# Light attention by whole token tiles, and a clock rule with fitted weights in the planner

## The chip, the core and the metric

The kernel runs on one core of a Trainium2 chip. A core has TensorE (PE; its weight loads are shown as PEld), VectorE (DVE), ScalarE (ACT), GpSimd (POOL) and SyncE (SP, which issues most DMAs). TensorE writes into PSUM, eight banks of 128 partitions by 512 float32 columns; VectorE or ScalarE copy the results out ("evict" them) into SBUF before TensorE can use them as operands or a bank can take the next tile. The metric is the device time of one execution in microseconds; the time of a kernel is the median of several executions.

## The reference

A macaron block on `x` of 8 sequences, 1024 tokens, 256 features, all float32: half a mixture of experts, attention, half a mixture of experts again.

```python
x = x + 0.5 * ffn(layernorm(x))
x = x + attn(layernorm(x))
x = x + 0.5 * ffn(layernorm(x))

def ffn(x):                      # 8 experts, hidden 128, the best two of each token
    logits = x @ router_w + router_b
    w = top-2 of softmax(logits), normalised
    return sum over experts of w * (gelu(x @ W1 + b1) @ W2 + b2)

def attn(x):                     # 8 heads of 64
    # light: windows of 64 tokens, each looks at itself and its two neighbours
    q, k, v = split(layernorm(x) * ln_g + ln_b) @ wqkv_l
    light = softmax(q k^T / 8 over 192 keys) v @ wo_l
    # heavy: the 256 best tokens by x.rt_q look at the 256 best by x.rt_kv
    heavy = softmax(hq hk^T / 8) (hv) @ wo_h, put back at the queries' places
    return light + heavy
```

## The kernel before

All eight sequences go through three stages: the first experts, attention, the last experts. Sequence 0 (first experts) and sequence 7 (last experts) compute all eight experts for every token (`dense`); the others sort their tokens by expert in DRAM, gather them in slots of 128 (`xp`, an indirect DMA from GpSimd), fetch the slot's expert weights (`wt`, 256 KB from SyncE) and compute one expert for a slot: transposes into `pt`, eviction to `xTe`, first layer into `ph`, GELU into `act`, second layer into `po`, eviction to `yp`. Different sequences' stages run at once: while one is in attention, others are in their experts.

Light attention (`light`, L1895) goes over 8 tiles of 128 tokens (two windows) of a sequence and, for each, over two groups `g` of four heads. `scores_light` (L1486) multiplies queries and keys of a group into `sim` (a tile of two PSUM banks, two such tiles take turns) with matmuls on 64 by 64 parts of the array, and `soften` (L1408) makes the softmax: negative maximum on VectorE (`nmax`), four exponentials on ScalarE (`a`, with sums `asum`), a reciprocal, and the scaling of `a` on VectorE or GpSimd. `values_light` (L1523) then works on one group: four transposes of the window's own keys into `pa`, evicted to `at` (512 columns); two transposes of the other keys into half of a bank `pb`, evicted to `bt` (256 columns); the products with the values into half of a bank `pav`, the own keys on 128 by 64 parts of the array and the neighbours' on 64 by 64 parts; and the eviction of that half (256 columns) to `loT`. After both groups `finish` multiplies `loT` by the output weights (`lo`), adds `ha` and stores to `h_b`. The calls stand one group behind the scores: scores of a group, then values of the group before. `prepare(t+1)` loads the next tile's `ha` and the neighbours' values `vside`.

SBUF tiles are taken in turn from rings: pool `two` has two buffers for each tag, `three` three, `one` one (`Plan.pool`, L301). Four of the eight PSUM banks hold the `sim` tiles, the other four are given to all other tiles (`bank`).

The order of the instructions is not the program's order. The program is run once with every call recorded; a planner (`Plan`, from L289) builds the dependences, orders the recorded calls by a list schedule with a cost for each (`Op.cost`, `Engine.work`), picks the engine for evictions and scalings (`copy`, `affine`, `scale`) and the PSUM bank for each tile, and repeats this for some rounds with ranks from the end. `schedule` (L517) has a small model of TensorE's clock in `run` (L538): in windows of `GATE` = 3413 ns the clock is full or half, by the busy share of the window before; before the change every busy nanosecond counts alike:

```python
busy = clock[2] / GATE
clock[0] = 1.0 if busy > (0.93 if clock[0] < 1 else 0.52) else 0.5
```

The program's order matters for the rings and for the first ranks. It is set by `PLACES` (L77): every stage has a start and an end on a scale where sequence `b`'s light attention takes `b` to `b + 1`, and `PLACES` adds an offset to each. Because almost every call goes through the recorder, most instructions carry the line of its issue, L269; evictions that choose their engine carry L352, L362 to L367, scalings L377. Instructions are told apart by the names of their tiles.

Of the kernel before, what the change touches and what calls it, by code (L numbers as in the profile page):

```python
# [44 lines left out]
F32 = mybir.dt.float32  # L45
# [12 lines left out]
P = 128  # L58
# [18 lines left out]
PLACES = {  # L77
    0: (-0.182, -0.019),
    1: (0.014, 0.072),
    2: (0.088, 0.002),  # L80
    3: (0.444, -0.124),
    4: (-0.157, -0.245),
    5: (-0.045, -0.526),
    6: (0.377, -0.016),
    8: (-0.109, 0.000),
    9: (0.160, -0.078),
    10: (0.002, -0.129),
    11: (0.070, 0.254),
    12: (0.003, 0.003),
    13: (0.434, 0.082),  # L90
    14: (0.122, -0.024),
    15: (0.274, 0.222),
    16: (0.214, 0.139),
    17: (0.169, 0.000),
    18: (0.273, -0.045),
    19: (0.099, 0.049),
    20: (0.074, -0.435),
    21: (0.000, 0.117),
    22: (0.205, -0.014),
    23: (-0.072, -0.036),  # L100
    24: (-0.039, -0.018),
    25: (-0.013, 0.000),
    26: (0.055, 0.481),
    27: (-0.013, 0.068),
    28: (-0.016, 0.000),
    30: (0.000, 0.002),
    31: (0.000, 0.484),
    32: (0.000, 0.090),
    34: (-0.002, 0.015),
    36: (0.063, 0.000),  # L110
    37: (0.034, -0.012),
    38: (0.032, 0.032),
    39: (0.000, -0.362),
    40: (0.029, 0.010),
    41: (0.499, 0.498),
    42: (0.099, 0.231),
    43: (0.000, 0.020),
    44: (0.050, -0.164),
    45: (0.007, -0.066),
    46: (0.311, 0.028),  # L120
    47: (0.196, 0.228),
    48: (0.076, -0.023),
    49: (0.030, -0.083),
    50: (0.000, 0.068),
    51: (-0.049, -0.114),
    52: (0.025, 0.137),
    53: (0.005, -0.060),
    54: (0.066, -0.609),
    55: (0.019, -0.108),
    56: (0.030, 0.183),  # L130
    57: (0.236, 0.070),
    58: (0.064, 0.043),
    59: (0.047, -0.286),
    60: (0.034, 0.000),
    61: (0.050, 0.000),
    62: (-0.041, -0.014),
    63: (0.123, -0.043),
    64: (-0.124, -0.048),
    65: (-0.290, -0.365),
    66: (-0.097, 0.030),  # L140
    67: (0.024, -0.106),
    68: (-0.011, 0.032),
    69: (0.132, 0.030),
    70: (0.439, 0.061),
}

# [18 lines left out]
RATE = 270.0  # L165
TURN = 185
QUARTER = 29
GATE = 3413.0


# [59 lines left out]
class Engine:  # L230
# [43 lines left out]
    @staticmethod  # L274
    def work(method, out, ins, kw):

        rows, cols, n = ins[0].shape[0], free(ins[0]), free(out)
        if method == "transpose":
            return {"work": 109.5, "array": (128, 128)}
        if ins[0].dtype in (BF16, F16):  # L280
            return {"work": max(25, n / 2.4 + 5), "array": (128, 128)}
        array = (64 if rows <= 64 else 128, 64 if cols <= 64 else 128)
        if array == (64, 64):
            return {"work": 58 * n / 64, "array": array}
        t = max(n * 2 / 2.4, cols / 1.2) + 4
        return {"work": t if array != (128, 128) else 2 * t, "array": array}


class Plan:  # L289
# [227 lines left out]
    def schedule(self, before, after, rank):  # L517
# [17 lines left out]
        last_use = [0.0] * len(left)  # L535
        free_at = dict.fromkeys(range(self.banks), 0.0)

        def run(t, work):  # L538
            while work > 1e-6:
                while clock[1] + GATE <= t:  # L540
                    busy = clock[2] / GATE
                    clock[0] = 1.0 if busy > (0.93 if clock[0] < 1 else 0.52) else 0.5
                    clock[1] += GATE
                    clock[2] = 0.0
                step = min(work / clock[0], clock[1] + GATE - t)
                clock[2] += step
                t += step
                work -= step * clock[0]
            return t
# [28 lines left out]
        while len(result) < len(ops):  # L578
# [11 lines left out]
            if e == PE:  # L590
                changed = o.how["array"] != array
                array = o.how["array"]
                now[e] = run(t, takes + (TURN if changed else 0))
                done = now[e] + (170 if clock[0] == 1 else 230) + LATE
            else:
                now[e], done = t + takes, t + seen_after + LATE
# [125 lines left out]
def program(  # L722
# [200 lines left out]
    def bank(name):  # L923
        return pmm.tile([P, HALF], F32, name=name)
# [595 lines left out]
                score(*one_of)  # L1520
        return soften(sim, 3 * W, f"{n}_{g}")

    def values_light(a, vside, t, g, loT, n):  # L1523


        at = keys_first(a, OWN, f"{n}_{g}_0")

        pb = bank(f"pb_{n}_{g}")
        for c in range(2):
            pair = a[:, 2 * c : 2 * c + 2, :].rearrange("p j k -> p (j k)")  # L1530
            nc.tensor.transpose(pb[:, ts(c, P)], pair[:, P : 2 * P], ident)
        bt = two.tile([P, 2, P], F32, tag="bt", name=f"bt_{n}_{g}")
        evict(bt.rearrange("p c q -> p (c q)"), pb[:, : 2 * P])
        pav = bank(f"pav_{n}_{g}")
        beside = windows_beside(t)


        for c in range(2):
            for j in range(2):
                hh = (4 * g + 2 * c + j) * DH  # L1540
                nc.tensor.matmul(
                    pav[j * DH : (j + 1) * DH, ts(c, P)],
                    v[:, t, hh : hh + DH],
                    at[:, 2 * c + j, :],
                    start=(c == 0),
                    stop=False,
                )
# [17 lines left out]
        evict(loT[:, ts(g, 2), :].rearrange("p c q -> p (c q)"), pav[:, : 2 * P])  # L1565


    def pc_of(pr, i):
# [326 lines left out]
    def light(b):  # L1895
# [240 lines left out]
```

## Time and profile before

| | us |
|---|---|
| median of 6 runs | 1830.6 (1826.22 to 1843.93) |
| the profiled execution | 1832.0 |
| its span, first to last instruction | 1830.3 |
| TensorE, matmuls busy | 1676.4 |
| TensorE, weight loads busy (beside matmuls) | 1248.6 |
| VectorE busy | 1233.9 |
| ScalarE busy | 918.4 |
| GpSimd busy | 846.5 |

The mean clock granted to TensorE was 0.965 of full speed. Busy times are sums over one execution; engines work beside each other. In a group's line stand source line, engine, operation, output and inputs by the program's names, shapes, count, then busy time, mean nanoseconds of one, and idle time of the engine ahead of it with what ended it. In the tile names `atl` is light and `ath` heavy attention, `f` an expert stage, and the digit before it the sequence.

### The profile page before, as it was taken

To read this page: it belongs to the slowest core of one execution; us is meant where nothing else is said; L and a number is where in the kernel's file an instruction comes from. 1 tells how busy PE (TensorE), PEld (TensorE's weight loads), DVE (VectorE), ACT (ScalarE), POOL (GpSimd) and SP (SyncE) were. 2 spreads that over 40 slices of the span, in tenths; PEclk is the share of its full clock that TensorE was granted. 3 is DMA by queue.
4 is the path that set the end of the run, shared out by engine and by line. 5 is a ranking of instruction groups with operands and counts; after the bars stand their busy time and mean duration, and the time that the engine had idled before them with its cause. 6 is when DMAs were issued, how large, how long until landed. Compare 5 with 4: busy or idle time off the path is not lost.

```text
span 1830.3 us, 39317 instructions
## 1 busy us (share of the span) xinstructions
PE 1676.4 (92%) x13753; PEld 1248.6 (68%) x13753; DVE 1233.9 (67%) x3904; ACT 918.4 (50%) x2554; POOL 846.5 (46%) x733
## 2 busy tenths in 40 slices
PE   7899899999999998899999889889989998999897
PEld 5676567666767766667767566658767666677786
DVE  5778559873865486677556698648647695558746
ACT  1134456545755543555646345538636454455532
POOL 1054562464642235553565644546454635454433
PEclk8899899999999999999999999999989999999999
DMA  9467765244851234564775432537565425744264
GB/s 163 167 217 212 216 200 158 71 126 128 268 166 53 53 102 148 179 213 122 226 241 171 119 107 91 179 110 227 186 203 151 134 86 155 226 124 135 73 190 125
DMA packets 220134, 284.66 MB, mean 156 GB/s; under 512 B 53496, under 2 KB 160960, under 8 KB 219680
## 3 DMA queue, kind: packets, MB, share of 16 engines
q1 hardware_dynamic: 190992, 208.82, 36.7%
q0 software_dynamic: 28368, 73.31, 14.7%
q8 instruction: 109, 1.79, 0.4%
q14 instruction: 89, 0.73, 0.1%
q10 hardware_dynamic: 576, 0.02, 0.0%
HBM read 196.20 MB, written 80.61 MB: 151 GB/s over the span
## 4 chain that ended last, share of the span: by engine, by line
PE 71%; DVE 16%; issue 5%; ACT 2%; DMA 2%; another core or an unknown queue 2%; POOL 1%; DVEq 0%; POOLq 0%; SPq 0%; ACTq 0%
PE po_0f L269 3%; PE ph_0f L269 3%; PE po_2f L269 2%; PE po_6f L269 2%; PE po_4f L269 2%; PE ph_2f L269 2%; PE po_7f L269 2%; PE ph_7f L269 1%; PE ph_4f L269 1%; PE ph_6f L269 1%; PE pt_2f L269 1%; PE pt_4f L269 1%; PE pt_6f L269 1%; PE lo_6at L269 1%
## 5 line engine op out<-in xcount | busy, mean ns | idle before, releaser
L269 ACT ACT_TABLE_LOAD x89 | 114.2, 1283 | 2.7 <-DVE nmax_5atl L269 1.2
L269 POOL DMA_INDIRECT xp_2f<-y_2f,token_2f x78 | 82.6, 1059 | 63.2 <-PE pt_2f L269 24.2
L269 POOL DMA_INDIRECT xp_6f<-y_6f,token_6f x62 | 64.4, 1039 | 68.7 <-PE pt_6f L269 43.2
L269 POOL DMA_INDIRECT xp_4f<-y_4f,token_4f x62 | 67.4, 1087 | 41.1 <-PE pt_4f L269 14.8
L269 POOL DMA_INDIRECT xp_0f<-y_0f,token_0f x39 | 41.5, 1064 | 41.7 <-PE pt_0f L269 20.9
L269 PE MATMUL po_2f<-wt_2f,act_2f 128*128 128x256 f32 x156 | 47.5, 395 | 7.0 <-issue 5.4
L269 PEld LDWEIGHTS ph_2f<-xTe_2f,wt_2f 128*128 128x128 f32 x312 | 42.2, 198 | 6.0 <-issue 4.1
L269 PE MATMUL ph_2f<-xTe_2f,wt_2f 128*128 128x128 f32 x312 | 46.0, 284 | 0.0
L269 POOL DMA_INDIRECT xp_1f<-y_1f,token_1f x23 | 24.7, 1076 | 42.6 <-PE pt_1f L269 14.8
L269 DVE SCALAR_TENSOR_TENSOR x_last<-po_7f,weight_7f,x_last 128x256 f32<-128x256 f32 x64 | 28.4, 478 | 21.2 <-PE po_7f L269 18.7
L269 PE MATMUL po_0f<-experts,act_0f 128*128 128x256 f32 x128 | 37.0, 430 | 5.4 <-DVE x_0at L269 5.4
L269 ACT ACTIVATE act_0f<-ph_0f,b_sb 128x512 f32<-128x512 f32 x16 | 11.0, 688 | 57.6 <-PE ph_0f L269 57.6
L377 POOL TENSOR_TENSOR a_7atl<-a_7atl,asum_7atl 128x768 f32<-128x768 f32 x14 | 21.0, 1503 | 38.4 <-DVE asum_7atl L269 20.0
L377 POOL TENSOR_TENSOR a_2atl<-a_2atl,asum_2atl 128x768 f32<-128x768 f32 x10 | 14.8, 1475 | 50.4 <-DVE asum_2atl L269 31.9
L269 PEld LDWEIGHTS ph_4f<-xTe_4f,wt_4f 128*128 128x128 f32 x248 | 33.7, 195 | 6.2 <-issue 4.6
L269 PE MATMUL ph_4f<-xTe_4f,wt_4f 128*128 128x128 f32 x248 | 36.5, 282 | 1.3 <-issue 1.1
L269 PEld LDWEIGHTS po_0f<-experts,act_0f 128*128 128x128 f32 x128 | 27.0, 219 | 15.4 <-DVE x_0at L269 6.2
L269 PEld LDWEIGHTS po_2f<-wt_2f,act_2f 128*128 128x128 f32 x156 | 24.6, 198 | 18.2 <-issue 12.2
L269 PE MATMUL po_6f<-wt_6f,act_6f 128*128 128x256 f32 x124 | 35.9, 383 | 1.2 <-issue 1.2
L269 PE MATMUL ph_6f<-xTe_6f,wt_6f 128*128 128x128 f32 x248 | 35.0, 278 | 2.1 <-issue 1.3
L269 PEld LDWEIGHTS ph_6f<-xTe_6f,wt_6f 128*128 128x128 f32 x248 | 32.5, 191 | 6.3 <-issue 3.5
L269 PE MATMUL po_4f<-wt_4f,act_4f 128*128 128x256 f32 x124 | 36.7, 387 | 0.0
(1547 smaller groups left out, 5889.8 us busy)
## 6 DMA issues: line engine op xcount, KB each, us to landing
wt_2f<-wpk SPq DMA_DIRECT2D x78, 256.5 KB
wt_4f<-wpk SPq DMA_DIRECT2D x62, 256.5 KB
wt_6f<-wpk SPq DMA_DIRECT2D x62, 256.5 KB
wt_0f<-wpk SPq DMA_DIRECT2D x39, 256.5 KB
ys_2f<-yp_2f SPq DMA_DIRECT2D x38, 256.0 KB
ys_4f<-yp_4f SPq DMA_DIRECT2D x30, 256.0 KB
ys_6f<-yp_6f SPq DMA_DIRECT2D x30, 256.0 KB
o<-h_b SPq DMA_DIRECT2D x56, 128.0 KB
```

The lines of the kernel that those rows point to most:

```text
L269: op = Op(self.plan, engines, lambda _: issue(*args, **kw), outs, ins, kind, **how)
L377: return getattr(nc, engine).tensor_tensor(dst, dst, by, op=ALU.mult)
```

## The change

`values_light` takes both groups of a token tile at once: `pb`, `bt` and `pav` hold all eight heads (512 columns), `loT` is evicted once; `at` stays one for each group. `bt` has one buffer in place of two. The planner's clock model gets a weight `live` for each kind of TensorE work (transposes 1.15, matmuls on parts of the array 1.0, small router matmuls 0.25, others by their columns), turns of the array count nothing, and the thresholds become 0.85 (to wake) and 0.5 (to keep). Most entries of `PLACES` have new values; the rings of SBUF buffers are as they were.

```diff
--- before.py
+++ after.py
@@ -77,70 +77,72 @@
...
-    2: (0.088, 0.002),
...
+    2: (0.093, 0.007),
...
-    12: (0.003, 0.003),
...
+    12: (-0.134, -0.134),
...
+    29: (0.005, 0.000),
...
-    39: (0.000, -0.362),
...
+    39: (0.158, -0.362),
...
-    65: (-0.290, -0.365),
...
+    65: (0.512, 0.433),
...
-    67: (0.024, -0.106),
-    68: (-0.011, 0.032),
...
+    67: (0.024, -0.354),
+    68: (0.069, -0.482),
...
@@ -165,6 +167,7 @@
 RATE = 270.0
 TURN = 185
 QUARTER = 29
+WAKES, KEEPS = 0.85, 0.5
 GATE = 3413.0
 
 
@@ -276,14 +279,18 @@
 
         rows, cols, n = ins[0].shape[0], free(ins[0]), free(out)
         if method == "transpose":
-            return {"work": 109.5, "array": (128, 128)}
+            return {"work": 109.5, "live": 1.15, "array": (128, 128)}
         if ins[0].dtype in (BF16, F16):
-            return {"work": max(25, n / 2.4 + 5), "array": (128, 128)}
+            work = max(25, n / 2.4 + 5)
+            return {"work": work, "live": n / 2.4 / work, "array": (128, 128)}
         array = (64 if rows <= 64 else 128, 64 if cols <= 64 else 128)
         if array == (64, 64):
-            return {"work": 58 * n / 64, "array": array}
+            return {"work": 58 * n / 64, "live": 1.0, "array": array}
         t = max(n * 2 / 2.4, cols / 1.2) + 4
-        return {"work": t if array != (128, 128) else 2 * t, "array": array}
+        if array != (128, 128):
+            return {"work": t, "live": 1.0, "array": array}
+        live = n * 4 / 2.4 / (2 * t) if n > 16 else 0.25
+        return {"work": 2 * t, "live": live, "array": array}
 
 
 class Plan:
@@ -535,15 +542,15 @@
         last_use = [0.0] * len(left)
         free_at = dict.fromkeys(range(self.banks), 0.0)
 
-        def run(t, work):
+        def run(t, work, live):
             while work > 1e-6:
                 while clock[1] + GATE <= t:
                     busy = clock[2] / GATE
-                    clock[0] = 1.0 if busy > (0.93 if clock[0] < 1 else 0.52) else 0.5
+                    clock[0] = 1.0 if busy > (WAKES if clock[0] < 1 else KEEPS) else 0.5
                     clock[1] += GATE
                     clock[2] = 0.0
                 step = min(work / clock[0], clock[1] + GATE - t)
-                clock[2] += step
+                clock[2] += step * live
                 t += step
                 work -= step * clock[0]
             return t
@@ -590,7 +597,7 @@
             if e == PE:
                 changed = o.how["array"] != array
                 array = o.how["array"]
-                now[e] = run(t, takes + (TURN if changed else 0))
+                now[e] = run(run(t, TURN if changed else 0, 0), takes, o.how["live"])
                 done = now[e] + (170 if clock[0] == 1 else 230) + LATE
             else:
                 now[e], done = t + takes, t + seen_after + LATE
@@ -1520,39 +1527,39 @@
                 score(*one_of)
         return soften(sim, 3 * W, f"{n}_{g}")
 
-    def values_light(a, vside, t, g, loT, n):
-
-
-        at = keys_first(a, OWN, f"{n}_{g}_0")
-
-        pb = bank(f"pb_{n}_{g}")
-        for c in range(2):
-            pair = a[:, 2 * c : 2 * c + 2, :].rearrange("p j k -> p (j k)")
-            nc.tensor.transpose(pb[:, ts(c, P)], pair[:, P : 2 * P], ident)
-        bt = two.tile([P, 2, P], F32, tag="bt", name=f"bt_{n}_{g}")
-        evict(bt.rearrange("p c q -> p (c q)"), pb[:, : 2 * P])
-        pav = bank(f"pav_{n}_{g}")
+    def values_light(both, vside, t, loT, n):
+
+        ats = [keys_first(a, OWN, f"{n}_{g}_0") for g, a in enumerate(both)]
+
+        pb = bank(f"pb_{n}")
+        for g, a in enumerate(both):
+            for c in range(2):
+                pair = a[:, 2 * c : 2 * c + 2, :].rearrange("p j k -> p (j k)")
+                nc.tensor.transpose(pb[:, ts(2 * g + c, P)], pair[:, P : 2 * P], ident)
+        bt = one.tile([P, KI, P], F32, tag="bt", name=f"bt_{n}")
+        evict(bt.rearrange("p c q -> p (c q)"), pb)
+        pav = bank(f"pav_{n}")
         beside = windows_beside(t)
 
 
-        for c in range(2):
+        for c in range(KI):
             for j in range(2):
-                hh = (4 * g + 2 * c + j) * DH
+                hh = (2 * c + j) * DH
                 nc.tensor.matmul(
                     pav[j * DH : (j + 1) * DH, ts(c, P)],
                     v[:, t, hh : hh + DH],
-                    at[:, 2 * c + j, :],
+                    ats[c // 2][:, 2 * (c % 2) + j, :],
                     start=(c == 0),
                     stop=False,
                 )
-        for c in range(2):
+        for c in range(KI):
             for w in beside:
                 for j in range(2):
                     r = slice(j * DH, (j + 1) * DH)
-                    hh = (4 * g + 2 * c + j) * DH
+                    hh = (2 * c + j) * DH
                     q = c * P + w * W
                     if w == j:
-                        vs = vside[r, 2 * g + c, :]
+                        vs = vside[r, c, :]
                     else:
                         vs = v[r, t + 2 * w - 1, hh : hh + DH]
                     nc.tensor.matmul(
@@ -1560,9 +1567,9 @@
                         vs,
                         bt[r, c, w * W : (w + 1) * W],
                         start=False,
-                        stop=(c == 1 and w == beside[-1]),
+                        stop=(c == KI - 1 and w == beside[-1]),
                     )
-        evict(loT[:, ts(g, 2), :].rearrange("p c q -> p (c q)"), pav[:, : 2 * P])
+        evict(loT.rearrange("p c q -> p (c q)"), pav)
 
 
     def pc_of(pr, i):
@@ -1942,22 +1949,21 @@
         prepare(0)
         waiting = None
         for t in range(NT):
+            assert written[0] == b and (t < 3 or written[1] == b)
+            if waiting is not None:
+                values_light(*waiting)
+                light_done[0] += 2
+                finish(t - 1, waiting[3])
+            both = [scores_light(t, g, f"{n}l{t}") for g in range(2)]
+            yield
+            if t + 1 < NT:
+                prepare(t + 1)
             loT = two.tile([P, KI, P], F32, tag="loT", name=f"loT_{n}_l{t}")
-            for g in range(2):
-                assert written[0] == b and (t < 3 or written[1] == b)
-                a = scores_light(t, g, f"{n}l{t}")
-                if waiting is not None:
-                    values_light(*waiting)
-                    light_done[0] += 1
-                    if g == 0:
-                        finish(t - 1, waiting[4])
-                if g == 0 and t + 1 < NT:
-                    prepare(t + 1)
-                waiting = (a, sides[t], t, g, loT, f"{n}l{t}")
-                yield
+            waiting = (both, sides[t], t, loT, f"{n}l{t}")
+            yield
         values_light(*waiting)
-        light_done[0] += 1
-        finish(NT - 1, waiting[4])
+        light_done[0] += 2
+        finish(NT - 1, waiting[3])
         if b not in EARLY:
             add_heavy(b, h_b[b])
         yield
```

More of the change, by code (lines that the diff above doesn't have):

```diff
@@ L79 @@
     1: (0.014, 0.072),
-    2: (0.088, 0.002),
-    3: (0.444, -0.124),
+    2: (0.093, 0.007),
+    3: (0.395, -0.124),
     4: (-0.157, -0.245),
     5: (-0.045, -0.526),
-    6: (0.377, -0.016),
+    6: (0.343, -0.122),
+    7: (0.000, -0.021),
     8: (-0.109, 0.000),
     9: (0.160, -0.078),
-    10: (0.002, -0.129),
-    11: (0.070, 0.254),
-    12: (0.003, 0.003),
[L90 to L97, printed above, removed]
+    10: (0.086, -0.129),
+    11: (0.079, 0.231),
+    12: (-0.134, -0.134),
+    13: (0.242, 0.043),
+    14: (0.266, 0.347),
+    15: (0.325, 0.193),
+    16: (0.293, 0.060),
+    17: (0.076, -0.108),
+    18: (0.203, -0.068),
+    19: (0.232, 0.090),
+    20: (0.152, -0.384),
     21: (0.000, 0.117),
-    22: (0.205, -0.014),
-    23: (-0.072, -0.036),
+    22: (0.265, -0.009),
+    23: (0.081, -0.221),
     24: (-0.039, -0.018),
-    25: (-0.013, 0.000),
+    25: (0.002, 0.000),
     26: (0.055, 0.481),
@@ L105 @@
     28: (-0.016, 0.000),
-    30: (0.000, 0.002),
-    31: (0.000, 0.484),
+    29: (0.005, 0.000),
+    30: (0.043, 0.045),
+    31: (0.011, 0.484),
     32: (0.000, 0.090),
[L109 to L112, printed above, removed]
-    39: (0.000, -0.362),
-    40: (0.029, 0.010),
+    34: (0.001, -0.046),
+    36: (0.198, 0.124),
+    37: (-0.031, -0.012),
+    38: (0.073, 0.038),
+    39: (0.158, -0.362),
+    40: (0.021, 0.002),
     41: (0.499, 0.498),
@@ L119 @@
     45: (0.007, -0.066),
[L120 to L128, printed above, removed]
-    55: (0.019, -0.108),
[L130 to L134, printed above, removed]
+    46: (0.271, -0.012),
+    47: (0.196, 0.324),
+    48: (0.076, -0.014),
+    49: (0.010, -0.012),
+    50: (-0.019, -0.003),
+    51: (0.017, -0.103),
+    52: (0.018, 0.130),
+    53: (0.012, -0.039),
+    54: (0.056, -0.610),
+    55: (0.019, -0.108),
+    56: (0.003, 0.402),
+    57: (0.233, -0.017),
+    58: (0.396, 0.041),
+    59: (0.047, -0.205),
+    60: (0.036, 0.001),
     61: (0.050, 0.000),
-    62: (-0.041, -0.014),
-    63: (0.123, -0.043),
-    64: (-0.124, -0.048),
-    65: (-0.290, -0.365),
+    62: (-0.103, 0.080),
+    63: (0.115, -0.051),
+    64: (-0.010, 0.056),
+    65: (0.512, 0.433),
     66: (-0.097, 0.030),
-    67: (0.024, -0.106),
-    68: (-0.011, 0.032),
-    69: (0.132, 0.030),
+    67: (0.024, -0.354),
+    68: (0.069, -0.482),
+    69: (0.075, 0.079),
     70: (0.439, 0.061),
```

## The prediction

> **What bounds the kernel now.** I read the page from the top: the span, the busy shares, the granted clock and the chain of waits; then the list of TensorE's waits, the groups of instructions kept apart by shape, and single windows of the clock.
>
> ```profile
> span 1830.3 us, 39317 instructions
> PE 1676.4 (92%) x13753; PEld 1248.6 (68%) x13753; DVE 1233.9 (67%) x3904; ACT 918.4 (50%) x2554; POOL 846.5 (46%) x733
> PEclk8899899999999999999999999999989999999999
> PE 71%; DVE 16%; issue 5%; ACT 2%; DMA 2%; another core or an unknown queue 2%; POOL 1%; DVEq 0%; POOLq 0%; SPq 0%; ACTq 0%
> L269 ACT ACT_TABLE_LOAD x89 | 114.2, 1283 | 2.7 <-DVE nmax_5atl L269 1.2
> ```
>
> TensorE is the bound: 92% busy, 71% of the chain. VectorE is next, with 16% of the chain; ScalarE and GpSimd hardly set the end. The mean granted clock is 0.965; the clock's own records hold 23 stretches at half, 129.4 us together, so at most 64.7 us are lost there. Time in which neither a matmul nor a weight load runs sums to 147.9 us. Eight of these waits are longer than 4 us (41.8 us, 5.2 each); some of them in the list of waits:
>
> ```profile
> PE pt_0f L269 <- DVE y_0f L269: 8.8, 1, 8.8
> PE pav_5atl L269 <- ACT act_4f L269: 4.6, 1, 4.6
> PE pb_2atl L269 <- ACT at_2atl L352: 4.4, 1, 4.4
> PE lk_4at L269 <- ACT kT L352: 4.2, 1, 4.2
> ```
>
> They have no common cause: each is once, at another tile. The rest of the idle time is many short waits, of the kind "a PSUM bank is not evicted yet".
>
> **The change part by part.** The sum is made against the profiled execution, 1832.0 us (span 1830.3 and 1.7 around it), 1.4 over the median of 1830.6.
>
> *Evictions in light attention.* There are 128 half tiles (8 sequences, 8 token tiles, 2 groups); each had one copy of 256 columns for `bt` and one for `loT`. The change makes 64 and 64 copies of 512.
>
> ```profile
> L352 ACT COPY at_6atl<-pa_6atl 128x512 f32<-128x512 f32 x14 | 8.1, 589 | 3.7 <-PE pa_6atl L269 3.0 <-issue 0.7
> L352 ACT COPY loT_5at_l<-pav_5atl 128x256 f32<-128x256 f32 x15 | 5.5, 373 | 14.2 <-PE pav_5atl L269 13.7
> L352 DVE COPY at_4atl<-pa_4atl 128x512 f32<-128x512 f32 x7 | 4.8, 682 | 0.2 <-PE pa_4atl L269 0.2
> L352 DVE COPY bt_6atl<-pb_6atl 128x256 f32<-128x256 f32 x11 | 4.5, 418 | 4.4 <-PE pb_6atl L269 3.3 <-PE pa_6atl L269 1.0
> ```
>
> One copy of 512 costs less than two of 256: 589 against 746 ns on ScalarE, 682 against 836 on VectorE. In the order of the built kernels VectorE falls from 95 copies of 256 to 51 of 512 (39.4 to 34.8 us), ScalarE from 161 to 77 (60.2 to 45.4). With all other copies and scalings that the planner moved between engines, each at its own row's mean, VectorE has 16.1 us less work, ScalarE 12.7 less (8 of its 90 table loads are gone, 8 x 1.283 = 10.3), GpSimd 3.7 less. Of the VectorE work I take its chain share in the middle of the run, about 20%: -3.2 us (bounds 0 and -16.1). ScalarE at its 2%: -0.3 (bounds 0 and -12.7). Its cover is TensorE's work; without it the whole 12.7 would count. GpSimd: 0, it is 46% busy and 1% of the chain.
>
> *TensorE's own work.* The same 8,284 matmuls and transposes, so no gain there. A change of the array's tile size costs about 100 ns over the usual spacing (medians 93 to 113 by kind, 56.7 us in all); the order has 391 of them before and 393 after: +0.2. The whole tile does not save turns, since the planner had already put the two groups' side windows together.
>
> *PSUM banks.* This is where I see the gain. I laid the trace's matmuls along the built order, gave each its usual spacing (109 ns a transpose, 2 x 216 for 256 float32 columns, and so on), and asked for each tile how much TensorE work lies between the last write to its bank's former tile and its own first write; what the start came late over the spacing is the wait. Under 0.6 us of cover the mean wait was 420 ns, at 0.8 to 1.0 it was 180, at 1.2 to 1.5 it was 90, over 2 us under 20. The change halves the number of `pb` and `pav` tiles, so bank reuses fall from 1,808 to 1,680, and those with under 1.2 us of cover from 299 to 201. By banks alone this is -13.8 us. Counting each matmul once, by the tighter of its bank and its freshly evicted operand, it is -8.4: reads of a fresh operand get slightly tighter elsewhere (GELU to second layer under 1.2 us: 84 to 112), though `loT` improves (33 of 128 reads had under 0.8 us, now none of 64). I take -8.4; bounds 0 (the wait only passes to the next operand) and -13.8. Idle time also costs clock: 64.7 us lost beside 147.9 idle is 0.44 us for each, so 8.4 becomes 12.1.
>
> *The clock rule* moves no instruction by itself; it changes the planner's times, hence the order. Is it right? Three windows show what it adds:
>
> ```profile
> 1088.50:1091.90 3.40, 3.40 (x35) 2.91 (x34) 3.40 (x18) 1.97 (x7) 0.33 (x1) 1.00 0.03 7
> 1091.90:1095.30 3.40, 3.40 (x10) 2.60 (x10) 3.40 (x7) 0.03 (x1) 1.56 (x1) 0.51 0.00 0
> 1668.80:1672.20 3.40, 2.88 (x30) 2.71 (x32) 2.54 (x9) 2.35 (x12) 1.45 (x1) 1.00 0.96 300
> 1672.20:1675.60 3.40, 3.40 (x30) 2.74 (x28) 0.83 (x3) 0.59 (x1) 1.49 (x2) 0.50 0.98 348
> 1675.60:1679.00 3.40, 3.40 (x87) 3.31 (x83) 2.43 (x4) 0.37 (x1) 0.00 (x0) 1.00 0.58 169
> ```
>
> The columns are window, length, busy time and count of PE, PEld, DVE, ACT, POOL, clock, DMA. TensorE is busy all of 1088.5 to 1091.9, yet the clock is 0.51 next: 16 of the 35 matmuls are the router's, with 8 columns each. The new weight of 0.25 for these says why. But the new order does little with it: of 34 router groups 17 stand unmixed, 19 before. Three such windows (74.8, 1088.5, 1668.8) led to 10.2, 3.4 and 3.4 us at half, 8.5 us lost; 2/19 of it is -0.9 (bounds 0 and -8.5).
>
> The rule gives transposes 1.15. The window from 1672.2 is half transposes (1.97 of 3.40 us busy), and the clock is back at 1.00 after it. [...]
>
> *What is moved.* `prepare(t+1)` comes behind both groups' scores, with its DMAs on SyncE's queue: one load of `ha`, and two copies into `vside` that take 0.61 us each to issue (median of 14). In the built order at least 13.0 us of TensorE's work lie between what releases a `vside` copy and its first matmul, 7.5 before: 0. The queue's first 23 rows are the same in both orders, so the attention weights' eight loads, which `PLACES` moves by 0.8 of a sequence, go out where they did: 0. All else that `PLACES` moves, by some tenths of a sequence, can only make or unmake long waits. One long wait costs 5.2 us and the half clock behind it (129.4 / 23 / 2 = 2.8), 8.0 in all. I have no reason for more or fewer of them: 0, bounds three fewer (-24) and three more (+24).
>
> Sum: 1832.0 - 3.2 - 0.3 + 0.2 - 12.1 - 0.9 = 1815.7; less the 1.4 between the profiled execution and the median, **1814 us**, 0.9% faster.
>
> **The rivals.**
>
> *The gain is absorbed.* Banks come free earlier, but the next wait in line, on VectorE's softmax work, ends at the same time. For it: VectorE's 35 us stretches on the chain (275 to 366, 641 to 732). Against: thin bank reuses lie all over the run. Then only VectorE's 3.2 and the half of the bank term remain: about 1823 to 1830.
>
> *The tied groups make TensorE wait: slower.* One `pb` and one `pav` now need the softmax of both groups, and the second group's scaling may stand in GpSimd's queue (1.5 us each, behind gathers of 1.06 us). Before, TensorE stood idle for GpSimd's `a` ahead of `pb` and `pa` nine times, 6.2 us. For it: the smallest TensorE work between a group's scores and its first transpose falls from 5.7 to 4.0 us, while the softmax takes 0.95 + 4 x 0.40 + 0.17 + 1.5 = 4.2. Against: the tenth percentile rises from 7.3 to 8.6 us. It decides from 0.34 us a tile (64 x 0.34 = 22 us, which lifts 1814 over 1840), or from three long waits. Likely then 1840 to 1855; at 0.45 us a tile, 1843.
>
> *More is gained.* The better clock rule lets the planner avoid three long waits: 1814 - 24 = 1790. Against: the order gives no sign of it.
>
> **How the numbers follow.** I give the forecast 0.48 (own range 1800 to 1828), absorbed 0.09, slower 0.28, more gained 0.15. What a measurement of this kernel can tell from no change is about 0.5%, 9.2 us: faster is under 1821.4, slower over 1839.8. Of the forecast's 0.48, 0.38 lies under 1821.4. Faster 0.38 + 0.15 = 0.53; same 0.10 + 0.09 = 0.19; slower 0.28. The range runs from 1782 (the lower bounds of the VectorE, ScalarE, bank and clock terms together, nearly) to 1848.
>
> **What would show it.** In the new profile: `bt` and `loT` copies of 512 near 590 and 685 ns, 64 of each; about 82 table loads; VectorE busy near 1218 us, ScalarE near 906; TensorE's time with nothing running near 139 us; half clock near 122 us. I am wrong if idle time or half clock grow, above all if `pa` and `pb` wait for `a` longer than 6 us in sum, or if the count of waits over 4 us is not eight.

## The result, and the profile after

The change makes the kernel slower by a little: 1851.4 us (median of 20 runs, 1845.7 to 1860.9) beside 1836.8 us for the kernel before on the same chip (median of 46 runs, 1821.5 to 1846.3), a ratio of 1.0087 [1.0069, 1.0105]. (Ratios here and below are of means, so they differ a little from the quotients of the medians; in brackets the 95% interval.)

The page of the changed kernel, with the span, the busy times, the granted clock in 40 slices, and the group of ScalarE's table loads (count, busy time and mean of one, idle time ahead):

```profile
span 1853.5 us, 39164 instructions
PE 1684.0 (91%) x13753; PEld 1253.1 (68%) x13753; DVE 1215.4 (66%) x3842; ACT 906.8 (49%) x2483; POOL 837.2 (45%) x730
PEclk8899999999999999899999989999989999999999
L272 ACT ACT_TABLE_LOAD x81 | 103.9, 1283 | 5.2 <-DVE nmax_1atl L272 3.8
```

And the light evictions in the same kernel, groups kept apart by shape (lines of the code stand 3 or 7 later than before):

```profile
L359 ACT COPY loT_2at_l<-pav_2atl 128x512 f32<-128x512 f32 x8 | 4.7, 585 | 17.5 <-PE pav_2atl L272 17.3
L359 ACT COPY bt_3atl<-pb_3atl 128x512 f32<-128x512 f32 x4 | 2.4, 595 | 0.3 <-issue 0.3
L359 DVE COPY bt_7atl<-pb_7atl 128x512 f32<-128x512 f32 x6 | 4.1, 690 | 3.7 <-remote 3.0 <-PE pb_7atl L272 0.5
```

VectorE and ScalarE do less, as worked out: 18.5 and 11.6 us less busy, 8 table loads gone. But TensorE stands idle longer. Its list of waits (line, what it waited for: us in total, times, longest):

```profile
PE po_0f L272 <- DVE x_0at L272: 9.6, 2, 9.0
PE po_6f L272 <- ACT act_6f L272: 7.6, 4, 2.7
PE lo_4at L272 <- issue: 6.3, 1, 6.3
PE pd_7at L272 <- DVE ha_6at L272: 5.1, 1, 5.1
PE po_4f L272 <- ACT act_4f L272: 3.2, 2, 2.7
```

`pb_2atl <- at_2atl` and `lk_4at <- kT`, 4.4 and 4.2 us before, are gone; in their place the experts' second layer (`po`) waits for GELU (`act`) several times. The place where the gain was expected shows it. What stood idle ahead of `pb` of sequence 2 (all engines that touch it; time and times), before:

```profile
  ACT at_2atl L352: 9.2, 2
  PE pb_2atl L269: 7.1, 7
  POOL a_2atl L377: 4.4, 3
```

and after:

```profile
  PE pb_2atl L272: 3.9, 2
  issue: 1.1, 3
```

The waits for `at` and for GpSimd's `a` have gone; what is left is `pb`'s copier waiting for TensorE. Not all of this is the bank's gain, though: the 9.2 us are one wait of 4.4 us, counted for matmuls and weight loads, and the experiments will show that it had another cause. The same view of `po` of sequence 6 goes the other way; before:

```profile
  PE po_6f L269: 12.1, 15
  ...
  ACT act_6f L269: 0.7, 3
```

and after:

```profile
  ACT act_6f L272: 11.2, 6
  issue: 9.6, 12
  PE po_6f L272: 8.2, 12
```

(weight loads and matmuls are counted one by one, so a wait of both counts twice).

Both kernels were profiled again later, so that chance differences between executions can be told from real ones. For a sum over the whole kernel I gave every matmul its usual spacing, as in the prediction, and called "lateness" what its start came later than that (half clock included):

| us | before, twice | after, three times (the last two are `again` and `after_again`) |
|---|---|---|
| span | 1830.3, 1835.4 | 1853.5, 1851.8, 1855.0 |
| neither matmul nor weight load runs | 147.9, 148.7 | 163.2, 161.1, 159.6 |
| in half clock | 129.4, 143.1 | 136.5, 146.3, 145.6 |
| lateness of all matmuls | 222, 227 | 242, 240, 243 |
| - first write to light's `pb` | 15.3, 15.9 | 1.1, 0.7, 0.8 |
| - first write to light's `pav` | 18.1, 18.0 | 11.1, 10.9, 13.5 |
| - first write to `lq`, `lk`, `lv` | 19.3, 20.5 | 11.8, 7.9, 7.4 |
| - first write to `po` (experts, second layer) | 21.7, 20.4 | 33.8, 35.0, 31.4 |
| - light scores `sim`, but the first | 10.5, 15.0 | 23.9, 24.4, 23.1 |
| - first write to `lo` | 9.3, 9.8 | 18.0, 15.1, 18.2 |
| - other own-key products in light's `pav` | 6.6, 7.1 | 14.6, 13.6, 14.9 |

So the first writes to light attention's `pb` and `pav` come 21 us less late (4.4 of them are the one wait of `pb_2atl`), and more than that was paid elsewhere, in every execution. The experiments ask who took it: one of the three parts, the mere fact that the plan is another, or something that the new plan runs into.

### The profile page after: what moved, and what is told of

Its sections match the earlier page's. It is cut to its first block, busy times and chain, and to the rows that moved or that the text cites. A ratio compares the mean times of both kernels' runs of the same rounds, so it can differ in the third digit from the quotient of the medians.

```text
span 1853.5 us, 39164 instructions
## 1 busy us (share of the span) xinstructions
PE 1684.0 (91%) x13753; PEld 1253.1 (68%) x13753; DVE 1215.4 (66%) x3842; ACT 906.8 (49%) x2483; POOL 837.2 (45%) x730
## 3 DMA queue, kind: packets, MB, share of 16 engines
q0 software_dynamic: 28368, 73.31, 14.9%
## 5 line engine op out<-in xcount | busy, mean ns | idle before, releaser
L272 POOL DMA_INDIRECT xp_4f<-y_4f,token_4f x62 | 64.7, 1043 | 47.1 <-PE pt_4f L272 22.6
L384 POOL TENSOR_TENSOR a_1atl<-a_1atl,asum_1atl 128x768 f32<-128x768 f32 x11 | 16.1, 1464 | 52.6 <-DVE asum_1atl L272 50.4
L272 PEld LDWEIGHTS po_0f<-experts,act_0f 128*128 128x128 f32 x128 | 25.3, 207 | 18.4 <-DVE x_0at L272 11.6
L272 ACT ACTIVATE act_2f<-ph_2f,wt_2f 128x128 f32<-128x128 f32 x78 | 24.4, 366 | 24.3 <-PE po_2f L272 9.7
L384 POOL TENSOR_TENSOR a_7atl<-a_7atl,asum_7atl 128x768 f32<-128x768 f32 x12 | 17.9, 1493 | 40.4 <-DVE asum_7atl L272 23.9
```

What stands on the lines that cost most here:

```text
L272: op = Op(self.plan, engines, lambda _: issue(*args, **kw), outs, ins, kind, **how)
L384: return getattr(nc, engine).tensor_tensor(dst, dst, by, op=ALU.mult)
```

## The experiments

### One part alone, and one part taken out

Each of the six kernels holds some of the diff's hunks: the whole tiles (`values_light`, `light`), the clock rule (`live`, `WAKES`, `KEEPS`), the places (`PLACES`). `f_tile_only`, for instance:

```diff
-    def values_light(a, vside, t, g, loT, n):
+    def values_light(both, vside, t, loT, n):
...
-            for g in range(2):
...
+            both = [scores_light(t, g, f"{n}l{t}") for g in range(2)]
```

`f_clock_only`:

```diff
-                    clock[0] = 1.0 if busy > (0.93 if clock[0] < 1 else 0.52) else 0.5
+                    clock[0] = 1.0 if busy > (WAKES if clock[0] < 1 else KEEPS) else 0.5
...
-                clock[2] += step
+                clock[2] += step * live
```

`f_places_only` has the `PLACES` lines alone; `f_places_clock`, `f_tile_clock` and `f_tile_places` have two parts each.

> The kernel before with the whole token tiles alone (old places, old clock rule). If the tied groups cost the time (rival 'slower'), it is at least 0.8% over the kernel before, ratio 1.008 or more, and TensorE waits for a ahead of pa and pb over 6 us. If the structure is a gain of the size that I worked out for the banks (8 to 14 us), ratio 0.992 to 0.996 and the waits at the first write to pb fall by about 13 us. If every new plan scatters by luck, anything from 0.99 to 1.015.

> The kernel before with the new clock rule alone (old places, half tiles). If the clock rule costs the time, ratio 1.008 or more and more half clock than 129 us. If it helps as meant, half clock under 122 us and a ratio under 1. If it is neutral and only luck of the plan acts, 0.99 to 1.015.

> The kernel before with the new places alone (half tiles, old clock rule). If the new places are what costs, ratio 1.008 or more, with more long waits of TensorE (over 2 us: 51 us before, 66 after the whole change). If they fit only together with the two other parts, also slower, while pairs with them are not. Luck alone: 0.99 to 1.015.

> The whole change without the whole token tiles (half tiles, new places, new clock rule). If the tied groups are the cost, this is back at 1.000 or under. If places or clock are, it stays at 1.008 or more.

> The whole change with the old places (whole tiles, new clock rule). If the new places are the cost, 1.000 or under; if tiles or clock are, 1.008 or more.

> The whole change with the old clock rule (whole tiles, new places). If the clock rule is the cost, 1.000 or under; if tiles or places are, 1.008 or more.

| parts | before there, us | this, us | ratio |
|---|---|---|---|
| tiles | 1693.9 | 1728.7 | 1.0182 [1.0137, 1.0226] |
| clock rule | 1693.9 | 1709.3 | 1.0085 [1.0057, 1.0113] |
| places | 1693.9 | 1731.3 | 1.0210 [1.0151, 1.0268] |
| places, clock rule | 1693.9 | 1719.6 | 1.0139 [1.0102, 1.0176] |
| tiles, clock rule | 1855.8 | 1870.4 | 1.0057 [1.0031, 1.0083] |
| tiles, places | 1855.8 | 1864.4 | 1.0052 [1.0027, 1.0077] |

Every part alone makes it slower, and taking any part out leaves it slower. The parts don't add up either: places alone cost 2.1%, with the clock rule 1.4%. No part is the culprit. Two of the parts alone, at 1.018 and 1.021, also lie above the 0.99 to 1.015 that I had given to luck of the plan, and the last two ratios lie between the bounds that I had set for and against a culprit. The first four ran on a chip on which the kernel before takes 1694 us; that is taken up below.

### A new plan without a change

If each new plan loses, one for no reason must lose too. These kernels alter one constant of the planner by a hair, which means nothing for the chip, but its greedy choices cascade and much of TensorE's order is another. `j_` kernels start from the kernel before (half tiles), `k_` kernels from the changed one; `again` is the changed kernel itself.

```diff
-LATE, LATE_DMA = 150, 500
+LATE, LATE_DMA = 152, 500
...
-RATE = 270.0
+RATE = 272.0
...
-TURN = 185
+TURN = 186
...
-SWITCH = 1295
+SWITCH = 1300
```

(one line for each: `_late`, `_rate`, `_turn`, `_switch`).

> The whole change once more, beside kernels that differ in nothing but the plan. Every theory: ratio near 1.009 if it does not depend on the chip; if the chip matters (the kernel before took 1694 us on one chip and 1856 on another), it may differ, and then only ratios of one call are to be compared.

> The kernel before with the planner's allowance for a signal 2 ns longer (152 for 150): a new plan without any meaning. If the plan before is a lucky or selected one and any new plan lands higher (theory of the plan's luck), ratio 1.003 to 1.02, as the six mixtures of the change's parts did (1.0052 to 1.021). If the parts of the change themselves cost the time, this stays within 0.997 to 1.003.

> The kernel before with the planner's DMA rate at 272 for 270: a second new plan without meaning. Luck of the plan: 1.003 to 1.02. Parts of the change cost the time: 0.997 to 1.003.

> The whole change with 152 for 150 in the planner's signal allowance. Luck of the plan: anywhere within about 1% of the whole change, as likely under it as over it. If the change's structure or clock rule sets the time, within 0.3% of the whole change.

> The kernel before with one planner constant (TURN, the planner's price of an array turn) at 186 for 185: no instruction is added or left out, but the planner's greedy choices cascade and much of TensorE's order is another. Theory (the 0.9% is the price of any new plan, since the plan before is a favourable one): 1.005 to 1.025 of the kernel before, as the two earlier re-plans gave 1.005 and 1.0248. Rival (the 0.9% belongs to the change's own structure): 0.997 to 1.003, and the 1.0248 was one unlucky plan.

> The kernel before with the planner's price of a table load (SWITCH) at 1300 for 1295: again a new plan and nothing else. Theory: 1.005 to 1.025. Rival: 0.997 to 1.003. A ratio below 0.995 would say that the plan before is no better than the average of its neighbours, and that the theory falls.

> The changed kernel with TURN at 186 for 185: the same structure as the change, another plan. With j_turn on the same chip it compares the structures when both are planned anew. If the structure is a gain that one favourable plan hides (bank waits 12 us less, work on VectorE and ScalarE 16 and 13 us less): 0.985 to 0.997 of j_turn on the mean of the two pairs. If it is neutral: within the spread of plans, 0.99 to 1.01. If the structure is the loss: 1.005 or more above the mean of the re-plans of the kernel before.

> The changed kernel with the planner's rate (RATE) at 272 for 270, the same constant that made the kernel before 2.48% slower. If a re-plan's price comes from the constant itself (a rate of 272 misjudges the transfers), this one is slower than the changed kernel by about 2% too: 1.025 to 1.035 of the kernel before. If it is chance of the plan: 1.002 to 1.015, the spread that the changed kernel's plans have shown (1.0054 to 1.0087).

| | before there, us | half tiles | whole tiles |
|---|---|---|---|
| the change again | 1836.3 | | 1.0064 [1.0026, 1.0101] |
| LATE 152 | 1836.3 | 1.0050 [1.0018, 1.0082] | 1.0054 [1.0024, 1.0084] |
| RATE 272 | 1836.3 | 1.0248 [1.0185, 1.0311] | |
| RATE 272 | 1696.3 | | 1.0156 [1.0120, 1.0193] |
| TURN 186 | 1696.3 | 1.0088 [1.0053, 1.0123] | 1.0195 [1.0159, 1.0231] |
| SWITCH 1300 | 1696.3 | 1.0205 [1.0168, 1.0242] | |

All seven meaningless plans lose, by 0.5 to 2.5%. With the six above and the change itself (taken at 1.0087), 14 of 14 plans are slower than the plan before. Their mean is 1.0146 for the seven with half tiles and 1.0112 for the seven with whole tiles, against a standard deviation of 0.007 from plan to plan in each. These means mix two kinds of chips. Where the kernel before takes 1694 to 1696 us, five plans with half tiles have a mean of 1.0145 and three with whole tiles 1.0178; on the slower chips it is two of 1.0050 and 1.0248 beside four of 1.0052 to 1.0087. So the plan before is a favourable one, and the structure, on equal footing, gains or loses nothing that this spread lets one see. That it is favourable because its constants were chosen with that very plan at hand is a guess; no run tells. Some single expectations were less clear: `k_late` lies within 0.3% of `again`, as it should if the structure sets the time, and within 1%, as it should if the plan does; `j_rate` lies above the range given to chance, and `k_rate` just above it, though far from the 1.025 to 1.035 expected if the constant itself did harm. On the chip that ran both structures twice, whole tiles come out at 1.003 of half tiles, which `k_turn`'s expectation calls neutral.

The bank term can be checked on equal footing too. On the chips where the kernel before takes 1694 to 1696 us, the lateness of the first writes to light's `pb` and `pav` together is 17.7, 19.1, 23.2, 16.2 and 18.8 us in the five plans with half tiles (`j_turn`, `j_switch`, `f_clock_only`, `f_places_only`, `f_places_clock`) and 10.6, 9.8 and 9.5 in the three with whole tiles (`k_turn`, `k_rate`, `f_tile_only`): 9.0 us less in the mean, and no overlap. The saving belongs to the whole tiles. Yet the lateness of all matmuls is 106 to 131 us (mean 116) with half tiles and 115 to 122 (mean 119) with whole ones: what is saved at these banks is waited for somewhere else.

### Both kernels side by side

No edit: the two kernels as they are, one after the other on one chip.

> The kernel before, unchanged, profiled beside the changed one on the same chip: 0.998 to 1.002 of itself. Theory (its plan is a favourable one in the waits of TensorE): its profile has less idle TensorE and less half clock than every re-plan seen on a chip of the same kind, by 10 to 35 us in sum. Rival (it is faster for something that these waits don't show): idle and half clock within 5 us of the re-plans'.

> The whole change once more, beside the profile of the kernel before on the same chip. If the chip is one on which VectorE and ScalarE have no waits that end on no known releaser (the kernel before near 1695 us): theory, 1.010 to 1.020, since the re-plans of both structures gave 1.0085 to 1.021 there; rival (the loss belongs to the slower chips), 0.99 to 1.003. If it is one with such waits (near 1840 us): 1.004 to 1.011 as in the first two comparisons. In both: first writes to the light attention's score banks wait 10 us less in sum than in the kernel before, the experts' second layer more.

The kernel before took 1834.8 us, 0.999 [0.9959, 1.0021] of itself, the changed one 1851.0 us, 1.0084 [1.0055, 1.0113]: the third comparison of the change that says 0.6 to 0.9% slower. Their profiles are in the table of the result. Idle time of TensorE grew by 13.0 us in the mean, from 148.3 to 161.3. Every new plan that was profiled on the slower chips has more of it than the plan before (157 to 165 us); in half clock (136 to 164 us beside 129 and 143) the plan before doesn't stand out, so the expectation came true in part. Of the last expectation for the changed kernel, `po` is 11 us later in these two profiles as foreseen, and `pb` and `pav` together are 20 us less late, but the scores `sim` are later, not earlier.

The waits behind most of these 13 us have a common cause. In the kernel before, this is the timeline of TensorE, ScalarE, VectorE and GpSimd, one after the other, around the wait of `pb_2atl` for `at_2atl`, which the prediction listed (start, duration, instruction; in brackets the idle time ahead and what ended it; "remote" is a release by no engine or queue that the profile knows):

```profile
699.22 0.63 PE L269 MATMUL pa_2atl<-ident,a_2atl 128*128 128x128 f32 x4 [1.36 <-issue]
...
706.00 0.33 PE L269 MATMUL pb_2atl<-ident,a_2atl 128*128 128x128 f32 x1 [4.42 <-ACT at_2atl L352]
...
705.36 0.59 ACT L352 COPY at_2atl<-pa_2atl 128x512 f32<-128x512 f32 x1 [6.28 <-remote]
...
705.26 0.96 DVE L269 TENSOR_REDUCE nmax_2atl<-sim_2atl 128x4 f32<-128x768 f32 x1 [6.83 <-remote]
...
698.06 1.12 POOL L269 DMA_INDIRECT xp_0f<-y_0f,token_0f  x1 [0.30 <-issue]
699.49 1.02 POOL L269 DMA_INDIRECT xp_0f<-y_0f,token_0f  x1 [0.30 <-issue]
700.81 1.01 POOL L269 DMA_INDIRECT xp_0f<-y_0f,token_0f  x1 [0.30 <-issue]
702.12 1.01 POOL L269 DMA_INDIRECT xp_0f<-y_0f,token_0f  x1 [0.30 <-issue]
703.44 1.01 POOL L269 DMA_INDIRECT xp_0f<-y_0f,token_0f  x1 [0.31 <-issue]
```

The transposes into `pa` end at 699.85, the scores `sim_2atl` before that. The signal that both engines wait for is TensorE's, yet ScalarE's copy starts at 705.36 and VectorE's reduction at 705.26, 0.9 and 0.8 us after the last indirect gather of a row has ended on GpSimd (704.45). The trace's record of semaphores shows where the time went: the one that TensorE counts up has no update between 698.68 and 705.24, and then four within 0.2 us, though the products `lo` that follow `pa` ended at 701.58 too. TensorE's signals arrived late, all together. I call such a wait a hold. Of the changed kernel's new waits for `act`, the one of 2.70 us is one too (the same view of that kernel; the `ph_6f` that `act_6f` reads is done by 1763.2):

```profile
1766.79 0.37 PE L272 MATMUL po_6f<-b_s,sel_6f 96*128 96x256 bf16 x1 [2.70 <-ACT act_6f L272]
...
1766.11 0.62 ACT L272 ACTIVATE act_6f<-ph_6f,wt_6f 128x128 f32<-128x128 f32 x2 [3.67 <-remote]
...
1762.74 1.01 POOL L272 DMA_INDIRECT xp_6f<-y_6f,token_6f  x1 [0.30 <-issue]
1764.06 1.01 POOL L272 DMA_INDIRECT xp_6f<-y_6f,token_6f  x1 [0.31 <-issue]
```

Again the held engine starts 1.0 us after the end of the last gather (1765.07).

I counted every idle time over 0.4 us of VectorE, ScalarE or GpSimd that ends on "remote". The kernel before has 31 such holds, 94.5 us in sum; 29 of them end during a gather or within 1.2 us after one, and such moments fill about half of the span (46%, or 50% with the longest gathers counted too). TensorE's idle time inside holds, and up to 0.7 us after their end while the held engine works, is 42.0 and 41.0 us before, 49.1, 52.4 and 49.9 after; outside them it is 105.9 and 107.7, then 114.1, 108.7 and 109.7. So 9 of the 13 us are new exposure to holds, 4 lie elsewhere. That is so for this plan and not for every one: in `k_late` and `f_tile_clock` only 32.8 and 33.9 us of TensorE's idle time lie in holds, less than in the kernel before, and they are 0.5 and 0.6% slower all the same, with 157 and 164 us idle in all.

### The gathers taken away

The last two kernels keep the order on TensorE, VectorE and ScalarE, and load plain rows in place of every gather, from SyncE's queue:

```diff
             issue = getattr(getattr(self.plan.nc, self.name), method)
+            if method.startswith("indirect") and args[1] is None:
+                flat = self.plan.nc.sync.dma_start
+                issue = lambda out, _, src, *a, **k: flat(out, src[0:P, :])
```

> The kernel before, with the same order on TensorE, VectorE and ScalarE, but every gather that GpSimd issues as an indirect DMA (xp, got, the heavy queries' rows) is a plain load of the source's first 128 rows from SyncE instead, so tokens' rows are the wrong ones in the experts, the combination and heavy attention. On chips where the kernel before takes about 1840 us, 29 of its 31 waits of other engines that end on no known releaser (95 us in sum) end during such a gather or within 1.2 us after one, while such moments fill 46% of the span. Theory (GpSimd's gathers hold up the signals): at most 5 such waits, under 15 us in sum, and 0.92 to 0.97 of the kernel before. Rival (they only stand beside it): 20 to 40 such waits, 70 us or more, and 0.98 to 1.03. On a chip without such waits (the kernel before near 1695 us): 0.98 to 1.03 by both, which leaves it open.

> The same edit in the changed kernel. TensorE's idle time that lies inside such waits grew from 41.5 us to 50.5 us by the change, the rest of its idle time from 107 to 111. Theory (most of what the change lost on these chips is more exposure to such waits): with the gathers gone the two kernels come closer, n_after 0.995 to 1.006 of n_before. Rival (the loss is the new order's, whatever the gathers do): n_after 1.007 to 1.02 of n_before, as the re-plans were 1.0085 to 1.021 of the kernel before on chips without such waits.

The chip was one on which the kernel before takes 1864.2 us. Without gathers it takes 1669.2 us, 0.8977 [0.8911, 0.9042], the changed one 1673.8 us, 0.8989 [0.8926, 0.9052]. Its page:

```profile
span 1666.3 us, 38597 instructions
PE 1607.0 (96%) x13753; PEld 1218.9 (73%) x13753; DVE 1225.1 (74%) x3904; ACT 919.3 (55%) x2554; POOL 266.5 (16%) x190
PEclk8999999999999999999999999999999999999999
```

and the page of the changed kernel without gathers:

```profile
span 1676.1 us, 38444 instructions
PE 1610.9 (96%) x13753; PEld 1223.2 (73%) x13753; DVE 1203.5 (72%) x3842; ACT 907.4 (54%) x2483; POOL 265.4 (16%) x187
```

There is no hold in either trace. VectorE and ScalarE run the same instructions in the same order as before, and so does TensorE in 99% of the places (99.6% between two executions of the kernel before). TensorE's idle time falls from 148 to 54.8 us in the one and from 161 to 60.7 in the other, half clock from 136 to 44.8 and from 143 to 56.6. (The profiles with gathers come from other chips.) More came than was expected (0.92 to 0.97): idle time outside holds was 106 us before, and 54.8 is all that is left, so waits that I don't count as holds went too. Several things were taken away together, though: the time that GpSimd itself spends on gathers (it is busy 266.5 us in place of 846.5), the gathers' own latency, and the wait for GpSimd's scalings behind them; that the holds go with the gathers is shown, but not that all 195 us are holds.

The two kernels now differ by 1.0024 [0.999, 1.006] (means of four runs each, the interval worked out from their scatter): inside the theory's 0.995 to 1.006 and not inside the rival's 1.007 to 1.02. Without gathers the change loses nothing that can be measured, and gains nothing. This doesn't make holds the general price of a new plan: on the chips where no profile has a hold, all eight new plans lose 0.9 to 2.1%. Both orders were also made by a planner that counted on gathers, so neither is a plan for the kernels that ran here. The change's bank term is there: first writes to light's `pb` and `pav` are 20.8 us late in `n_before` and 8.4 in `n_after`. But first writes to `po` come 5.7 us later in sum, those to `pt` 4.6, heavy `pa` 2.2, and 11.8 us more are spent at half clock (5.9 us lost), which outweighs it.

## Why the prediction was wrong

*Evictions and engines: right in size, no gain to be seen.* Copies of 512 took 582 to 596 ns on ScalarE and 678 to 690 on VectorE (590 and 685 were named), 81 table loads (82), VectorE 1215.4 us busy (1218), ScalarE 906.8 (906). The -3.2 us for VectorE's chain share can't be told apart in any run; without gathers VectorE has 21.6 us less to do and the kernel is no faster.

*PSUM banks: the place right, the passing to the end wrong.* I took -13.8 us for the banks by themselves and -8.4 net of what freshly evicted operands take back. On equal footing the whole tiles save 9.0 us at the two banks, without gathers 12.4, which is the size of the first figure; the net saving, in the lateness of all matmuls, is nil. But the sum let the saving pass to the end of the kernel, with 44% on top for the clock (64.7 us lost beside 147.9 idle). It didn't: that lateness is the same for both structures (116 and 119 us). This is the rival "the gain is absorbed", to which I gave 0.09, and not through VectorE's softmax as I had it, but at many next operands of TensorE: `po`, `pt`, heavy `pa`. I had seen one of them in the built order (GELU to second layer under 1.2 us of cover: 84 to 112) and priced it, with all its like, at 5.4 us of the 13.8. The first writes to `po` alone came 12.4 us later in sum.

*The step that failed* is the one on `PLACES`: "All else that `PLACES` moves, by some tenths of a sequence, can only make or unmake long waits. ... I have no reason for more or fewer of them: 0". Waits over 4 us were indeed seven in place of eight (44.8 us beside 41.8). But those of 2 to 4 us rose from 9.3 to 21.8 us, and idle time as a whole by 13 us. Where my other terms gave -16 us, the kernel became 15 us slower. Zero is the fair price of a new plan only if the old one is no better than its neighbours. The plan before is better than all 14 others that ran, by 0.5 to 2.5%, so an edit that makes the planner choose anew has to expect a loss, whatever it was for. The one profile that I had doesn't show that. Why just this plan is better stays open.

*"They have no common cause"*, said of the eight long waits, was wrong in part. Three of them (13.8 us), and three of 2 to 4 us (9.3), lie in holds; in the changed kernel ten waits over 2 us do (33.3 us). The sign stood in the lines that I quoted: "another core or an unknown queue 2%" in the chain of waits, 35 us of a kernel on one core. I read past it. So the price of this new order on these chips had an ingredient that I never costed: how often a hand-over from TensorE falls among GpSimd's gathers.

*The clock rule*: the term was -0.9 us. Half clock went from 136 to 143 us in the mean, and alone the rule made the kernel 0.85% slower; like the others it was a new plan first of all. No run takes one of its weights or thresholds by itself. In the traces of the kernel before and the changed one, every stretch at half but the last, which the end of the records cuts, is one to four times 3.41 us long. In such windows at full clock TensorE's matmuls were busy for 43 and 34% of the time in the mean when a half one followed, for 94% in both kernels when none did. In the kernel before, none of the 32 full windows that transposes fill to 42 to 54% had a half one behind it. Three full windows that were busy for 85% or more did, those that the prediction names, each with 16 router matmuls; seven other windows with 16 of these kept the full clock.

*The tied groups make TensorE wait*: the time was right by luck (1840 to 1855 holds 1851), the mechanism was not. `pa` and `pb` wait 0.7 to 1.1 us for GpSimd's `a` in the three profiles of the changed kernel, 6.2 before; the test that I named, 6 us, refutes it. Its threshold was also added up wrongly: 22 us on top of 1814 are 1836 and not over 1840, which takes 0.41 us a tile. *More is gained* did not come. *Moved loads and array turns*: turns cost 60.3 us in place of 56.7; of TensorE's waits over 1 us none ends on a load of `ha` or `vside`, as 0 said.

## What to carry to other kernels

A kernel whose order comes out of a greedy planner has a spread of plans. Before a small structural gain is believed or given up, plan the old kernel anew a few times for no reason and compare the new one with that spread, not with the one plan that was kept. A wait removed from a busy engine need not shorten the kernel: here 9.0 us less at two banks left the lateness of all matmuls at 119 us beside 116. And a release that the profile can't name, on a kernel of one core, is a thing to be explained first: here the kernel without the gathers behind it was 195 us faster, while the change moved 15.

## What the runs showed of the hardware that was not expected

- *Gathers and signals.* While GpSimd works through a row of indirect gathers (1.02 us each in the median, 0.30 apart), finished work of TensorE can stay unseen by VectorE and ScalarE for microseconds: 27 to 43 holds in a profile, up to 8.6 us each, 93 to 137 us in sum, in all ten profiles from chips where the kernel before takes 1834 to 1856 us. In all 323 of them the signal that came late is TensorE's. A third end while a gather is running, a third 0.8 to 1.1 us after one, and none more than 1.6 us after one. With plain loads from SyncE there are none. By which path a gather holds up a signal is not shown. Both engines are held: in the hold at 705 us ScalarE stood idle for 6.28 us and VectorE for 6.83.
- *Chips.* On two other chips the same program takes 1694 and 1696 us, 8% less, and eight profiles taken there have no hold, though the gathers are as many and as long (559 indirect DMAs with a median of 1.02 us in `j_turn` and in the kernel before). What differs between these chips isn't known. A ratio from one kind of chip need not hold on the other: whole-tile plans cost 1.6 to 2.0% on the one and 0.5 to 0.9% on the other.
